# Dilated dynamic filters of layer 1 as matrix products within classes of pixels of equal row and column modulo 6

## The chip, the cores and the metric

The kernel runs on one core of a Trainium2 chip. The metric is device microseconds of one execution. Engines are named as in the profile: PE (TensorE matmul), PEld (its weight loads), DVE (VectorE), ACT (ScalarE), POOL (GpSimd), SP (SyncE, which here only issues DMAs).

## The reference

Four images of 256 channels and 48x48 pixels, all in float32, go through two residual layers. Layer 0 normalizes in groups, convolves 3x3, and applies attention with 8 heads of 32 channels over all 2304 pixels. Layer 1 is what the change concerns. Cut to its core (`gn` is the group-normalized input):

```
guidance = conv3x3(gn, W_cat)                    # 45 planes
outs = [gn]
for i, d in enumerate((1, 6, 12, 24, 36)):
    w = softmax(guidance[:, 9*i : 9*i+9], axis=1)     # 9 weights a pixel
    outs.append(sum over k of shift(gn, dy*d, dx*d) * w[:, k])   # k = (dy, dx), zero outside
y = conv1x1(concat(outs), W_scale)               # 6*256 -> 256 channels
x = x + batchnorm(y)          # statistics over all images
```

The nine weights of a dilation depend on the pixel and are the same for all channels.

## The kernel before, in words

A channel lies on a partition: 256 channels are two halves (`NH`) of 128. An image is cut into six chunks (`NCK`) of eight rows, 384 pixels (`CH`). An outer loop over `b` from 0 to 4 (L1624 onward) alternates two kinds of work. `dynamic_filters(b - 1, ...)` does layer 1 of one image; beside it, as a generator named `other`, runs `conv_qkv(b, ...)`, the convolution and q, k, v of the next image. Then `attention(b, ...)` follows alone. For the last image (`alone`) there is no `other`. I call the three stages with an `other` shared and the last one lone.

The schedule is written out by hand: each engine runs its instructions in program order. The order is chosen by a planner, `Clock` (L645), which holds a time for each engine and is told a cost for each step; `slot` (L663) gives the time at which a buffer is free, and `fill` (L1266) lets PE take filter steps, mixing matmuls from `queue`, or pieces of `other` until a given time. `conv` gives its input transforms (`inputs`, L731) to POOL for all images but the first.

Within `dynamic_filters`:

- `weights` (L1135) makes a chunk's 45 weight planes: a 3x3 convolution on PE (`pg`, L1148, 45 columns, two at a time in two column groups), copies to `lg`, transposes (`pt`), softmax on DVE and ACT (L1188 to L1205), transposes back (`pw`, L1210), a copy to `w` (one in the F32R type and a remainder added in its upper rows), and a store to the DRAM tensor `w_d` on ACT's DMA queue (L1221).
- For each tap (a dilation, a shift) the weight plane must stand on all 128 partitions. Either PE makes it, with a selector column as stationary operand, into a PSUM bank (`wb`, L1432), or the plane is loaded from `w_d` with a broadcasting DMA (`ws`, L1377, ACT's queue) and ACT copies it to PSUM (L1429). `share` and the planner decide; about three fifths go to PE.
- DVE multiplies the bank with the shifted image (`cat` at L1463 for the centre tap, `prod` at L1489 for the others) and POOL adds the product to `cat` (L1506, L1478). Some taps are split between DVE and POOL (L1471 to L1478). In the lone stage some products are mixed without being summed (`single`).
- `mix` (L1294) applies the 1x1 convolution: per dilation and chunk two output halves by two input halves on PE (`py`, L1303). `done` (L1316) copies a finished chunk to SBUF, takes its statistics and stores it to `y_d`.

Taps outside the image are cut away (`taps_of`, L1096). The pixels of a chunk are eight consecutive rows.

At the lone stage's second chunk `back` (L1740) loads the stored `y` and `x1` of earlier images, on SP's queue. `finish` (L1590) scales each image on ACT, adds `x1` on DVE and stores the result on SP's queue, chunk by chunk.

Of the kernel before, what the change touches and what calls it, by code (L numbers as in the profile page):

```python
# [8 lines left out]
F32 = mybir.dt.float32  # L9
# [27 lines left out]
CATS = 4  # L37
PRODS = 6
SLACK = 3000.0
SPLIT = 4500.0  # L40
BEHIND = 0.0
# [7 lines left out]
def conv_preact_kernel(  # L49
# [480 lines left out]
    w_d = tc.dram_tile([B, NCK, NG, CH], F32, name="w_d")  # L530
# [3 lines left out]
    with tc.tile_pool(name="w", bufs=1) as wpool, tc.tile_pool(  # L534
# [22 lines left out]
        pick = wpool.tile([P, NG], F32R, tag="pick", name="pick")  # L557


        e1 = wpool.tile([P, 2 * TPC, 2, 64], F32, tag="e1", name="e1")  # L560
        nc.gpsimd.memset(e1, 0.0)

# [8 lines left out]
        lg = wpool.tile([P, CH], F32, tag="lg", name="lg")  # L571
        nc.gpsimd.memset(lg, 0.0)
# [523 lines left out]
        def taps_of(c, n):  # L1096

            d = DILATIONS[n]
            moves = [(0, 0)] + [
                (sy, sx) for sy in (-1, 0, 1) for sx in (-1, 0, 1) if sy or sx  # L1100
            ]
            for sy, sx in moves:
                oy, ox = sy * d, sx * d
                y0, y1 = max(c * R, -oy), min(c * R + R, HH - oy)
                x0, x1 = max(0, -ox), min(WW, WW - ox)
                if y0 < y1 and x0 < x1:
                    yield 9 * n + 3 * (sy + 1) + sx + 1, oy, ox, y0, y1, x0, x1

        TAP_ELEMENTS = sum(
            NH * (y1 - y0) * (x1 - x0)  # L1110
            for c in range(NCK)
            for n in range(len(DILATIONS))
            for _, _, _, y0, y1, x0, x1 in taps_of(c, n)
        )

        def dynamic_filters(b, ao, chunk, norm, other, pools):


            ps_w, ps_y, ps_m, work1 = pools
            gn = pads[b % 2]  # L1120
            spent = [0.0]
# [12 lines left out]

            def weights(cs):  # L1135


# [4 lines left out]
                for at in range(0, 9 * NH, 3 if pair else 6):  # L1142
                    for i, k in ((at // 9, at % 9 + d) for d in range(3)) if pair else (
                        (0, at // 2 + d) for d in range(3)
                    ):
                        for s in range(2):
# [4 lines left out]
                                window(gn, ii, cc * R, k // 3 - 1, k % 3 - 1),  # L1151
# [12 lines left out]
                for t in range(TPC):  # L1164
                    if pair:
                        nc.tensor.transpose(
                            pt[:, t * P : (t + 1) * P], lg[:, t * P : (t + 1) * P], ident
                        )
                    else:

                        nc.tensor.matmul(
                            pt[:, t * P : t * P + NG], lg[:, t * P : (t + 1) * P],
                            pick.bitcast(F32), start=True, stop=True,
                        )
                lt = pt[:, : TPC * P].rearrange("p (t j) -> p t j", j=64)[:, :, :NG]
                step = 1 if pair else 2
                lt = lt.rearrange("p t (n k) -> p t n k", k=9)[:, ::step]
                ek, ek2 = (
                    e1[:, ::step, j, :NG].rearrange("p t (n k) -> p t n k", k=9) for j in range(2)
                )  # L1180
# [9 lines left out]
                yield 0.0  # L1190
# [7 lines left out]
                yield 0.0  # L1198
                nc.vector.reciprocal(sm, sm)
                clock("DVE", 330)  # L1200
                yield 0.0
                nc.vector.tensor_tensor(ek2, ek, each(sm), ALU.mult)
                clock("DVE", 700)
                yield 0.0
                nc.vector.tensor_tensor(ek, ek, each(sm), ALU.mult)  # L1205
                yield clock("DVE", 1100) + 150
                for s in range(len(cs)):
                    pw = misc(f"pw_{b}_{c + s}")
                    for t in range(TPC):
                        nc.tensor.transpose(  # L1210
                            pw[:, t * P : (t + 1) * P],
                            e1[:, 2 * t + s].rearrange("p a j -> p (a j)"),
                            ident,
                        )

                    w = work1.tile([P, CH], F32R, tag="w", name=f"w_{b}_{c + s}", bufs=3)
                    nc.scalar.copy(w, pw[:, :CH])

                    wf = work1.tile([NG, CH], F32, tag="wf", name=f"wf_{b}_{c + s}", bufs=1)
                    nc.scalar.copy(wf, pw[:NG, :CH])  # L1220
                    nc.scalar.dma_start(out=w_d[b, c + s], in_=wf)  # L1221
                    clock("ACT", 500)
                    yield clock("ACT", 480, clock("PE", 550))
                    nc.vector.tensor_tensor(
                        w[64:], pw[64:, :CH], w[64:].bitcast(F32), ALU.subtract
                    )
                    ready[c + s] = w
                    yield clock("DVE", 560, clock.t["ACT"]) + 150


            alone = b == B - 1
            prods = PRODS - alone
            ready = {}

            def warm(n):
                if alone:
                    busy(misc(f"warm_{b}_{n}"), n)


            while chunk < NCK:  # L1240
                project(b, chunk, ao, ps_y.tile([P, 2, 512], F32, tag="y", name=f"pp_{b}_{chunk}"), norm)
                chunk += 1
            table(AF.Sqrt)
            warm(4)
            run(2400)
            for at, _ in enumerate(norm.finish(misc)):
                run((600, 700)[at])
            table(AF.Exp)
            warm(3)

            for r0, r1 in ((0, 2 * R + 1), (2 * R + 1, HH)):
# [614 lines left out]
```

## Time and profile before

Three runs: 2863.04, 2856.90 and 2862.41 us; the median is 2862.41. The profiled execution is one execution; its span is given here, its own time outside the span is not recorded apart.

| | us |
|---|---|
| median of 3 runs (lowest, highest) | 2862.41 (2856.9, 2863.04) |
| span of the profiled execution | 2861.5 |
| opening: first convolution and q, k, v, to 149.4 | 149.4 |
| four attentions | 378.1, 383.9, 381.5, 377.0 |
| three shared stages | 300.3, 301.3, 300.5 |
| lone stage | 256.0 |
| finish | 33.5 |
| `wb` matmuls in the whole run | 553 records, busy 269.3 |
| `ws` loads | 355, 192 KB each, 3.2 to landing |

How to read it: a group's row gives the instruction's line, engine, tiles, shape and count, then busy time and mean, then idle time before it and what ended that. Busy time of a group is the union of its records, and records of matmuls overlap: an f32 matmul leaves two records, an F32R matmul one.

### The profile page before, as it was taken

Reading aid. Unit: us, or ns where it says so; the run is one execution under the profiler, and the core shown is the slowest. Engines: PE = TensorE matmul, PEld = TensorE weight load, DVE = VectorE, ACT = ScalarE, POOL = GpSimd, SP = SyncE. Lnnn points to the kernel's source line nnn. Section 1 sums busy time; section 2 is a strip of 40 time slices with the busy share of each in tenths; the row PEclk is TensorE's granted clock in tenths of the full one; section 3 lists DMA queues with packets and bytes.
Section 4 is the critical chain, followed back from the end, with each engine's and each line's share of the span. In section 5 each row is a group of like instructions: output and inputs, shape, how many; then the busy total and the mean of one; then the engine's idle time right before and its main releaser. Section 6 shows DMA issues by size and latency. Waiting matters only on the chain. (4 is left out here: it accounts for less than half of the span.)

```text
span 2861.5 us, 43939 instructions
## 1 busy us (share of the span) xinstructions
PE 2703.3 (94%) x16899; PEld 1188.5 (42%) x16899; DVE 2384.4 (83%) x2598; ACT 1707.9 (60%) x2186; POOL 1200.6 (42%) x1036
## 2 busy tenths in 40 slices
PE   7999999999999999999999999999999999998994
PEld 5622223556542222455662222355555222244562
DVE  6588989789878888878987888878986988887886
ACT  3488988422458888722337888852244988871224
POOL 2100010799840010299890010069985001006894
PEclk9999999999999999999999999999999999999997
DMA  5514454233353454333235454424323255435125
GB/s 205 146 34 101 105 106 103 63 115 88 86 120 84 100 106 100 80 90 109 84 86 107 99 105 106 100 68 112 95 77 90 67 106 112 100 81 220 57 74 209
DMA packets 161017, 292.87 MB, mean 102 GB/s; under 512 B 68888, under 2 KB 127072, under 8 KB 159392
## 3 DMA queue, kind: packets, MB, share of 16 engines
q0 software_dynamic: 25568, 135.18, 20.8%
q1 hardware_dynamic: 77776, 80.23, 9.9%
q10 hardware_dynamic: 57456, 74.58, 9.6%
q8 instruction: 135, 2.21, 0.3%
q14 instruction: 82, 0.67, 0.1%
HBM read 134.92 MB, written 32.33 MB: 58 GB/s over the span
## 5 line engine op out<-in xcount | busy, mean ns | idle before, releaser
L1008 DVE TENSOR_TENSOR acc<-acc,p 128x2048 f32<-128x2048 f32 (+1 forms) x572 | 1061.3, 1855 | 116.2 <-ACT p L972 64.8
L972 ACT ACTIVATE p<-se 128x1536 f32<-128x1536 f32 x648 | 938.6, 1448 | 0.0
L1506 POOL TENSOR_TENSOR cat<-cat,prod 128x752 f32<-128x752 f32 (+9 forms) x649 | 868.0, 1346 | 127.4 <-DVE prod L1489 81.3
L963 PE MATMUL so<-q,k 32*128 32x512 f32 (+1 forms) x1440 | 731.0, 595 | 20.1 <-ACT p L971 13.2
L963 PE MATMUL se<-q,k 32*128 32x512 f32 (+1 forms) x4320 | 739.8, 595 | 0.0
L992 PE MATMUL num<-p,vT 128*32 128x512 f32 (+1 forms) x5760 | 705.7, 562 | 4.4 <-ACT p L972 2.4
L1489 DVE TENSOR_TENSOR prod<-wb,pad 128x752 f32<-128x752 f32 (+9 forms) x675 | 474.8, 739 | 79.1 <-PE wb L1432 36.5
L971 ACT ACTIVATE p<-so 128x512 f32<-128x512 f32 x648 | 388.4, 599 | 195.0 <-PE se L963 83.1
L963 PEld LDWEIGHTS so<-q,k 32*128 32x128 f32 x1440 | 217.0, 184 | 539.4 <-ACT p L971 490.0
L1012 POOL DMA_DIRECT2D scratch<-p x124 | 105.6, 852 | 770.1 <-ACT p L972 536.4
L1429 ACT COPY wb<-ws 128x384 f32<-128x384 f32 (+3 forms) x335 | 156.7, 468 | 405.8 <-DVE prod L1489 200.3
L1303 PE MATMUL py<-cat,wsc 128*128 128x384 f32 x960 | 344.6, 490 | 17.5 <-POOL cat L1506 15.0
L992 PEld LDWEIGHTS num<-p,vT 128*32 128x32 f32 x5760 | 133.3, 108 | 479.6 <-issue 446.6
L1432 PE MATMUL wb<-w,pick 128*128 128x384 f32 (+3 forms) x553 | 269.3, 515 | 21.8 <-DVE prod L1489 14.5
L1010 POOL DMA_DIRECT2D scratch<-p x32 | 17.9, 559 | 571.3 <-ACT p L972 387.2
L963 PEld LDWEIGHTS se<-q,k 32*128 32x128 f32 x4320 | 227.6, 184 | 4.4 <-ACT p L972 4.1
L1303 PEld LDWEIGHTS py<-cat,wsc 128*128 128x128 f32 x960 | 174.9, 189 | 124.3 <-POOL cat L1506 30.7
L855 PE MATMUL pc<-cv_q,u 128*128 128x288 f32 x576 | 160.6, 412 | 8.9 <-DVE cv_q L746 6.3
L855 PE MATMUL pc<-cv_k,u 128*128 128x288 f32 x576 | 157.9, 410 | 2.9 <-ACT m L801 2.5
L1148 PE MATMUL pg<-pad,wcat 128*45 128x384 f32 x864 | 157.6, 497 | 3.1 <-DVE pad L595 2.9
L1432 PEld LDWEIGHTS wb<-w,pick 128*128 128x128 f32 x553 | 103.1, 190 | 120.6 <-DVE prod L1489 38.4
L888 PE MATMUL pq<-hid,wqkv 128*128 128x384 f32 x384 | 133.4, 488 | 5.9 <-DVE yt L790 4.8
(229 smaller groups left out, 2360.0 us busy)
## 6 DMA issues: line engine op xcount, KB each, us to landing
scratch<-p POOLq DMA_DIRECT2D x156, 768.0 KB, 5.7
ws<-w_d ACTq DMA_DIRECT2D x355, 192.0 KB, 3.2
pad<-in_x SPq DMA_DIRECT2D x14, 1152.0 KB, 15.5
u<-u_d SPq DMA_DIRECT2D x18, 768.0 KB, 5.3
x_d<-pad SPq DMA_DIRECT2D x48, 192.0 KB, 2.7
xst<-in_x POOLq DMA_DIRECT2D x36, 192.0 KB, 7.9
y_d<-y SPq DMA_DIRECT2D x15, 384.0 KB, 3.6
u_d<-u SPq DMA_DIRECT2D x6, 768.0 KB, 3.8
```

What stands on the lines that cost most here:

```text
L855: nc.tensor.matmul(m, u[:, h, kx, o * P : (o + 1) * P], halves[g][:, h, i, :, kx : kx + WW], start=(h == 0 and kx == 0), stop=(h == NH - 1 ...
L963: nc.tensor.matmul(dst[:, at : at + n], k_[r, g, m * P : (m + 1) * P], q[r, g, q0 : q0 + n], start=True, stop=True,)
L971: nc.scalar.activation(p[:, 0, :], s1, AF.Exp, scale=QS)
L972: nc.scalar.activation(p[:, 1:, :], s3, AF.Exp, scale=QS)
L992: nc.tensor.matmul(st["num"][r, at : at + n], vT[:, m, g * P + j * D : g * P + (j + 1) * D], p[:, j, at : at + n], start=(m == 0 and not s ...
L1008: nc.vector.tensor_tensor(st["acc"][:, js], other[:, js], p[:, js], ALU.add)
L1148: nc.tensor.matmul(pg[64 * s : 64 * s + NG, :CH], wcat[:, ii, k, :], window(gn, ii, cc * R, k // 3 - 1, k % 3 - 1), start=(i == 0 and k == 0),
L1303: nc.tensor.matmul(to, wsc[:, n * NH + i, o * P : (o + 1) * P], rhs(i), start=(n == 0 and i == 0), stop=(last and i == NH - 1),)
L1429: nc.scalar.copy(pw[:, : nr * WW], of[:, : nr * WW])
L1432: nc.tensor.matmul(pw[:, : nr * WW], pick[:, k : k + 1].to_broadcast([P, P]), w[:, l0 * WW : l1 * WW], start=True, stop=True,)
L1489: nc.vector.tensor_tensor(pv, wb, src, ALU.mult)
L1506: nc.gpsimd.tensor_tensor(dst, dst, pv, ALU.add)
```

## The change

**Which pixels belong together.** All far dilations (6, 12, 24, 36) are multiples of 6. A pixel's taps at those dilations all lie in the pixel's own class: rows equal modulo 6, columns equal modulo 6. A class is 8x8 = 64 pixels (`CLS`). A chunk is now every sixth row, so chunk `c` holds six whole classes; two classes make 128 rows, three such pairs (`PAIRS`) a chunk.

**Far dilations** (`far`). For a chunk the image is copied into class order (`own`), turned on PE (`xa`, `xb`: six transposes) and kept as `xT`, pixels on partitions. The weights go through DRAM: the store leaves zero margins in `w_d`, and four small loads per chunk (`loads`) fetch each plane displaced by its tap, so that a row of `wq` holds, for each source pixel, the weight with which it enters its target. Six small matmuls turn them (`wT`). Three predicated copies under masks (`along_x`) spread them over the eight columns of a class (`bmat`), three more (`along_y`) over its eight rows (`amat`): `amat` is then, for each class and dilation, a 64x64 matrix from source to target pixels. Per pair, four matmuls of 64 rows and 256 columns (4 dilations x 64 pixels) give the four dilations' sums, for two channel halves and two classes; the copies that bring them to SBUF (`moved`) go to ACT or DVE, whichever the planner's clock has earlier.

**The near dilation** (`near`) keeps taps: nine per chunk, all on whole rows, as the padded image is read past its edge. Their weights all come by broadcasting DMA and an ACT copy; there is no `wb` matmul. DVE multiplies, POOL adds.

**Order.** Generators `loads`, `far`, `near`, `filters` and `mixes` say when they are due; `drive` takes the first that is due at the clock of PE, and otherwise a piece of `other`. The mixing order in a chunk is the image itself, the four far dilations, the near one.

**Moved.** Weight stores, broadcasts and small loads are issued on SP's queue instead of ACT's. `lg`, `bmat` and `amat` are set to zero by POOL at the start of each image's stage. One half of the normalization goes to ACT. `own` shares its buffer with the chunk's output `y` in the shared stages. Masks are made once, at the start, by POOL. `finish` works on rows that are six apart, and stores images 2 and 3 after their sixth chunk. PSUM: 1 bank for broadcasts and 2 for `far` (lone stage: 2 and 3).

The diff, cut to its core:

```diff
-            ps_w, ps_y, ps_m, work1 = pools
+            ps_w, ps_k, ps_y, ps_m, work1, banks_w, banks_k = pools
...
+            def moved(dst, src, size, *after):
+                if clock.t["ACT"] <= clock.t["DVE"]:
+                    nc.scalar.copy(dst, src)
+                    return clock("ACT", 190 + 0.84 * size, *after)
+                nc.vector.tensor_copy(dst, src)
+                return clock("DVE", 160 + 1.05 * size, *after)
...
+            for t in (lg, bmat, amat):
+                nc.gpsimd.memset(t, 0.0)
...
-                                window(gn, ii, cc * R, k // 3 - 1, k % 3 - 1),
+                                shifted(ii, cc, k // 3 - 1, k % 3 - 1),
...
+                nc.scalar.copy(lg, pw[:, :CH])
...
+                    nc.sync.dma_start(
+                        out=w_d[c + s, :, MARGIN : MARGIN + CH], in_=lg[64 * s : 64 * s + NG]
+                    )
...
+            def loads():
...
+                    for n, d in enumerate(FAR):
...
+                        nc.sync.dma_start(out=t[9 * n : 9 * n + 9, :], in_=a)
...
+            def far():
+                for c in range(NCK):
...
+                    for k in range(STEP):
+                        rows = slice(CLS * (k % 2), CLS * (k % 2 + 1))
+                        at = 9 * NF * (k // 2)
+                        nc.tensor.matmul(
+                            bank[rows, at : at + 9 * NF], wq[:, k], ident[: 9 * NF, : 9 * NF],
+                            start=True, stop=True,
+                        )
...
+                    for t in range(3):
+                        nc.vector.copy_predicated(
+                            bmat,
+                            along_x[:, :, t, :].bitcast(mybir.dt.uint32).unsqueeze(1).to_broadcast(
+                                [P, PAIRS, 3 * NF, SIDE]
+                            ),
+                            wT[:, :, :, t].unsqueeze(3).to_broadcast([P, PAIRS, 3 * NF, SIDE]),
+                        )
+                        end = clock("DVE", 460, end)
...
+                        nc.vector.copy_predicated(
+                            amat,
...
+                        end = clock("DVE", 960)
...
+                    for p in range(PAIRS):
...
+                        for h in range(NH):
+                            for s in range(2):
+                                rows = slice(CLS * s, CLS * (s + 1))
+                                nc.tensor.matmul(
+                                    two[s][:, h * C : (h + 1) * C],
+                                    xT[rows, p, h * P : (h + 1) * P],
+                                    amat[rows, NF * p : NF * (p + 1)].rearrange(
+                                        "p n j i -> p (n j i)"
+                                    ),
+                                    start=True,
+                                    stop=True,
+                                )
+                        clock("PE", 950)
+                        for s in range(2):
...
+                            done_at = moved(
+                                dst, two[s].rearrange("p (k m) -> p k m", m=CLS), 512,
+                                clock.t["PE"],
+                            )
...
+            def near():
...
+                    fetch(number + WBS)
...
+                    nc.scalar.copy(pw[:, :CH], fetched[c, k][0])
...
+                    nc.gpsimd.tensor_tensor(cat, cat, prod, ALU.add)
...
-                        nc.tensor.matmul(
-                            pw[:, : nr * WW],
-                            pick[:, k : k + 1].to_broadcast([P, P]),
-                            w[:, l0 * WW : l1 * WW],
-                            start=True,
-                            stop=True,
-                        )
...
+            def mixes():
+                order = (0, *range(2, 2 + NF), 1)
+                for c in range(NCK):
+                    now[0] = c
+                    if alone and c == 1:
+                        back()
...
+            def drive(streams):
...
+                        if d <= clock.t["PE"]:
+                            due[j] = next(streams[j], None)
+                            break
+                        soonest = min(soonest, d)
+                    else:
+                        got = next(other, None)
...
+            streams = [
+                loads(), far(), near(), filters([(0,), (1,), (2, 3), (4, 5)]), mixes(),
+            ]
...
             for b, ty, tx in ((2, y_2, x1_2), (3, homes, x1_3)):
                 for c in range(NCK):
...
-                    nc.sync.dma_start(out=image_of(out, b)[:, :, cols], in_=ty[c])
...
+                for o in range(NH):
+                    for cols in (slice(0, N // 2), slice(N // 2, N)):
+                        nc.sync.dma_start(out=image(b, o)[:, cols], in_=tx[:, o, cols])
```

## The prediction

> **What bounds the kernel now.** I read the page's totals first, then busy time by stage, then the waits of a stage, then single stretches of the timeline.
>
> ```profile
> PE 2703.3 (94%) x16899; PEld 1188.5 (42%) x16899; DVE 2384.4 (83%) x2598; ACT 1707.9 (60%) x2186; POOL 1200.6 (42%) x1036
> ```
>
> PE carries the run. A limit is read by stage, though. The table cuts the span at the first score matmul of each attention and at its last projection; columns are PE, PEld, DVE, ACT, POOL busy, then PE clock, DMA share, GB/s.
>
> ```profile
> core 0: us, PE busy (x) PEld busy (x) DVE busy (x) ACT busy (x) POOL busy (x), PEclk, DMA share, GB/s
> 149.40:527.50 378.10, 370.98 (x3017) 105.71 (x3017) 331.04 (x218) 330.06 (x354) 40.75 (x46) 0.99 0.40 87
> 1211.70:1513.00 301.30, 286.20 (x1147) 178.02 (x1145) 248.57 (x396) 88.72 (x182) 272.12 (x211) 1.00 0.34 90
> 2572.00:2828.00 256.00, 232.85 (x922) 138.59 (x920) 201.87 (x327) 49.65 (x106) 206.37 (x166) 0.97 0.35 117
> 2828.00:2861.50 33.50, 0.00 (x0) 0.00 (x0) 23.70 (x31) 25.98 (x38) 0.00 (x0) 0.52 0.83 309
> ```
>
> The first row is an attention, which the change leaves alone (four of them, with the opening 149.4 us). The second is one of three *shared* stages: layer 1 of an image with layer 0 of the next on PE, PE 95% busy. The third is the *lone* stage, layer 1 of the last image with nothing beside it. The fourth is the finish. Only the last three kinds can change. Next, what PE waits for in a shared stage:
>
> ```profile
> PE py L1303 <- POOL cat L1506: 5.2, 8, 1.1
> PE wb L1432 <- DVE prod L1489: 3.2, 5, 1.1
> PE so L963 <- DVE bound L926: 2.0, 1, 2.0
> ```
>
> Idle is 15.1 us, 8.4 of it on tap sums and products: PE's own work sets the stage's length. Last, what one broadcast costs PE (start, length):
>
> ```profile
> 656.74 1.46 PE L1303 MATMUL py<-pad,wsc 128*128 128x384 f32 x4
> 658.03 2.74 PE L1303 MATMUL py<-cat,wsc 128*128 128x384 f32 x8
> 660.32 0.63 PE L1432 MATMUL wb<-w,pick 128*128 128x384 f32 x1
> 660.79 1.13 PE L855 MATMUL pc<-cv_q,u 128*128 128x288 f32 x4
> ```
>
> Start to start, 4 mixing records take 1.29 us, so 8 take 2.58; eight and one broadcast take 2.76. A broadcast adds 0.18 us, though its record says 0.63. Records overlap; starts are the measure. An f32 matmul leaves two records.
>
> [...] in attention 16 records of 32 rows and 256 columns, four heads side by side, take 1.07 us from 499.57 to 500.64 in slots of 0.21 to 0.32. [...] a POOL add of 128x600 goes from 1.46 to 2.14 us while DVE normalizes (1217 to 1226). [...]
>
> ```profile
> L1506 POOL TENSOR_TENSOR cat<-cat,prod 128x768 f32<-128x768 f32 x114 | 208.0, 1825 | 10.2 <-DVE prod L1489 1.5
> L1489 DVE TENSOR_TENSOR prod<-wb,pad 128x768 f32<-128x768 f32 x120 | 113.9, 949 | 12.5 <-ACT wb L1429 4.9 <-POOL cat L1506 3.9 <-PE wb L1432 3.0
> L1429 ACT COPY wb<-ws 128x384 f32<-128x384 f32 x304 | 146.8, 483 | 357.7 <-DVE prod L1489 181.5 <-DMA ws<-w_d 83.3 <-DVE cat L1463 47.0
> ```
>
> **PE in a shared stage.** What stays, by starts in gap-free stretches: 288 conv records at 0.2425 us (24 in 5.82) are 69.8; 96 qk at 0.3225 are 31.0; 72 v at 0.2175 are 15.7; 288 mixing at 0.3225 are 92.9; 216 filter records at 0.169 (36 in 6.08) are 36.5; transposes of logits and weights 5.6. Sum 251.5. Busy is 286.2, so 134 broadcasts with the switches around them hold **34.7 us**, all removed (134 x 0.18 = 24 is the floor).
>
> Added, per image: 18 groups of four K=64 matmuls, two row halves side by side. Each is four slots of 0.215 [...], like the attention stretch: 1.07, sum 19.3. Were the halves not parallel, it would be 8 slots, 1.9 each, 34.8. 36 transposes at 0.167 (18 `pw` records are 3.00 busy) are 6.0. 36 matmuls of 36 columns, 72 records at 0.1 (6 `pt` records start to start about 0.6), are 7.2. Sum **32.5**, between 27 and 51. Mixing is the same 144 matmuls. So -2 net.
>
> Waits: the 8.4 us on tap sums go; new ones stand on copies of the far results (three PSUM groups of a chunk pass through two banks). DVE falls to about 150 us of 300 and POOL from 272 to about 140 (48 adds of 1.83 and some 50 of conv inputs), so I take -2, between -8 and +15. POOL's queue: three memsets per image now stand ahead of the conv inputs, and wait for attention's buffers. Inputs begin at 1203 now; attention's last DVE step ends at 1207.1. With 1.3 us of memset (448 ns for 128x384) they begin at 1208.4 and the first conv matmul moves from 1211.6 to about 1214: +2 (0 to 3). ACT broadcasts fall from 88 to 54 and are hidden. A shared stage: -2; **three: -6** (-36 to +36).
>
> **The lone stage.** Here the chain counts. From 2572: PE's filter convolution ends near 15 us, `pw` at 20 as now; copy 0.5, store 1.8, four small loads' issues and landing about 5: the first `wT` at 28. Three predicated copies of 288 and three of 768 follow, priced as tensor_tensor of the size (0.45 and 0.95): 4.2; doubled they are 8.4; below that I see no reason for. With chunk 1's softmax between, far group 0 runs at 35. PE is full meanwhile: far groups with filters of chunks 2 and 3 to 50, mixing of far 0 (16 matmuls, 10.3, and transposes) to 62, filters of 4 and 5 (12.2) to 74, then far 1, near 0, own 1 and turning chunk 2 to 85.5.
>
> From then a chunk's period is the longer of two. PE: 10.3 + 2.6 + 2.6 of mixing, 3.2 far groups, 2 turning: 20.7. Chain: copies and statistics 5.3, then in DVE's order the next near products, whose 8 POOL adds take 14.6 behind a first product of 0.95, then half a mix 1.3, turning 2: **24.2**. Three periods reach 158; near, own and far mixing 14.2, the last far group 10, far mixing 10.3, near and statistics 4.6: end near **198 instead of 256: -58**. Bounds: PE alone -75; copies doubled on the chain in six chunks, -33.
>
> On SP's queue the weight broadcasts now stand behind 11.8 MB of loads that `back` issues at about 52 us (at the 420 GB/s that such loads reach at 2580 to 2610: 28 us). Chunk 2's are wanted at about 115: hidden; uncovered 28.
>
> **Finish and start.** ACT does about 27 us of scaling (25.98 now), but the last image's 2.36 MB go out after its sixth chunk instead of chunk by chunk: at 390 GB/s 6 us and a landing of 2 to 3, against 6.4 now from ACT's last end. Row: **+5** (2 to 8). At the start, 72 tiny POOL copies and 12 small stores lie in a POOL that is 27 us busy in 149: 0; uncovered they delay statistics by about 9 us that PE wants only at 123.
>
> **Sum.** 2861.5 - 6 - 58 + 5 = 2802.5 in the profiled execution; the median of the runs is 0.9 above its span: **2803 us**.
>
> **Rivals.**
> 1. The lone stage shrinks half as much: predicated copies at half speed, or `back`'s loads in the way. For: no row shows that copy; the queue is shared. Against: the cover of 60 us above. 256 to 228, total 2833.
> 2. The shared stages gain too: -34.7 in full against 27, and the 8.4 us of waits go. For: DVE and POOL have half their time free. -12 each: 2862.4 - 36 - 58 + 5 = 2773.
> 3. Slower: PE waits at every far group, because DVE's half of the copies stands in its queue behind up to two products (2 x 0.95 = 1.9). For: two banks, in-order queue. Against: ACT takes the other half, and conv matmuls stand between groups. 18 x 3 x 1.9 = 103, so 2906. It decides from 59/54 = 1.1 us a group.
>
> That the broadcasts stay is excluded: the new instruction order has no `wb` matmul.
>
> **Chances.** Forecast 0.50, rival 1 0.18, rival 2 0.18, rival 3 0.14. The range 2765 to 2850 takes in the first three and leaves out most of rival 3 and a tail. Within 0.2% (6 us, about what can be told from no change) 0.03, slower 0.13, faster 0.84, since rival 3 passes through no change when its wait is near 1.1 us.
>
> **What would show it.** Stages of 298 and 198 us and a finish of 38; PE busy in a shared stage near 284; far groups about 1.07 us; predicated copies of 0.45 and 0.95. Wrong if a far group takes 1.9, if the copies take double, if PE's waits in a shared stage exceed 25 us, or if the lone stage stands on `ws` landings.

## The result, and the profile after

The changed kernel takes 2794.07 us (median of 4 runs, 2793.82 to 2797.24). Beside it the kernel before took 2861.09 (4 runs, 2856.9 to 2863.04). The ratio is 0.9772, with a 95% interval of 0.9758 to 0.9786. The forecast was 2803, in a range of 2765 to 2850. The profiled execution has a span of 2791.9 us. First the page's totals.

```profile
PE 2647.6 (95%) x17122; PEld 1140.7 (41%) x17122; DVE 2024.1 (72%) x1948; ACT 1771.8 (63%) x2175; POOL 632.1 (23%) x583
```

PE still carries the run. Over the whole run it is 56 us less busy, DVE 360 and POOL 568. Now the stages. To compare them I cut both spans by one rule: a shared stage runs from the start of an attention's last projection to the next attention's first score matmul, and the lone stage ends where the scale of the final normalization starts (`ysc_f`). Rows of before cut in this way come first: the second shared stage, lone stage, finish. (The prediction's shared row was cut 1.5 us later.)

```profile
core 0: us, PE busy (x) PEld busy (x) DVE busy (x) ACT busy (x) POOL busy (x), PEclk, DMA share, GB/s
1211.20:1511.40 300.20, 285.10 (x1140) 177.97 (x1139) 248.57 (x396) 88.72 (x182) 272.55 (x212) 1.00 0.33 90
2571.60:2828.20 256.60, 233.25 (x923) 138.81 (x921) 202.03 (x328) 49.65 (x106) 206.37 (x166) 0.97 0.35 117
2828.20:2861.50 33.30, 0.00 (x0) 0.00 (x0) 23.53 (x30) 25.98 (x38) 0.00 (x0) 0.51 0.83 309
```

The same stages of the changed kernel:

```profile
1198.30:1490.40 292.10, 285.65 (x1253) 176.06 (x1251) 154.87 (x229) 102.74 (x175) 119.54 (x72) 1.00 0.33 81
2539.10:2752.30 213.20, 182.23 (x810) 98.00 (x808) 122.17 (x171) 68.62 (x113) 87.04 (x48) 0.95 0.41 128
2752.30:2791.90 39.60, 0.00 (x0) 0.00 (x0) 24.39 (x33) 26.81 (x41) 0.00 (x0) 0.53 0.70 271
```

In the shared stage PE is as busy as before (285.1, then 285.7), but its idle time went from 15.1 to 6.5 us. In the lone stage PE's work fell by 51 us and the stage by 43. The account of the span:

| | before, us | after, us | difference | forecast |
|---|---|---|---|---|
| opening | 149.4 | 149.8 | +0.4 | 0 |
| four attentions | 377.6, 384.3, 382.6, 377.3 | 376.5, 379.9, 380.1, 377.2 | -8.1 | 0 |
| three shared stages | 299.9, 300.2, 300.3 | 292.1, 292.1, 291.4 | -24.8 | -6 |
| lone stage | 256.6 | 213.2 | -43.4 | -58 |
| finish | 33.3 | 39.6 | +6.3 | +5 |
| span | 2861.5 | 2791.9 | -69.6 | -59 |

What PE waits for in the second shared stage after the change (total us, times, longest us):

```profile
PE pw L1244 <- DVE e L1240: 2.2, 2, 1.8
PE pg L1190 <- DVE pad L631: 1.4, 1, 1.4
PE pc L891 <- POOL cv_q L782: 1.2, 1, 1.2
PE xa L1307 <- ACT own L1163: 1.1, 1, 1.1
```

The rows on tap sums (5.2 us) and products (3.2) are gone, and so is the one on `bound` (2.0). No row on far results has come in their place. The end of the same stage tells more. Before the change PE ends it with the last tap sums of layer 1 and then has nothing to do until the bound is there:

```profile
1504.83 0.49 PE L1303 MATMUL py<-cat,wsc 128*128 128x384 f32 x1
1506.45 2.85 PE L1303 MATMUL py<-cat,wsc 128*128 128x384 f32 x8 [1.13 <-POOL cat L1506]
1509.13 0.28 PE L925 MATMUL pb<-qktop,hmat 128*128 128x2 f32 x2
1511.40 0.99 PE L963 MATMUL so<-q,k 32*128 32x512 f32 x1 [1.99 <-DVE bound L926]
```

After the change it ends with the next image's v matmuls, and the first scores follow at once:

```profile
1484.79 5.56 PE L945 MATMUL pv<-wqkv,hid 128*128 128x256 f32 x25
1490.19 0.28 PE L961 MATMUL pb<-qktop,hmat 128*128 128x2 f32 x2
1490.40 1.12 PE L999 MATMUL so<-q,k 32*128 32x512 f32 x2
```

Layer 1, with POOL busy for 272 of 300 us, used to end last; now layer 0 does, which is PE's own work.

In the lone stage most of the 51 us are mixing. Three rows give the instructions of one tile alone: the mixing (`py`) before, the broadcasts (`wb`) before, and the mixing after (length of the stage, then busy time and count of PE, PEld, DVE and ACT):

```profile
2571.60:2828.20 256.60, 163.73 (x496) 89.85 (x496) 1.13 (x2) 4.94 (x7) 0.97 0.35 117
2571.60:2828.20 256.60, 70.17 (x151) 27.97 (x151) 171.25 (x264) 33.16 (x71) 0.97 0.35 117
2539.10:2752.30 213.20, 102.87 (x288) 54.31 (x288) 1.13 (x2) 4.95 (x7) 0.95 0.41 128
```

Before, products of this stage were mixed without being summed first, so the mixing took 496 records; now it takes 288, as in a shared stage, which is 61 us less. The 151 broadcasts are gone too. Their records overlap those of their neighbours; what the other groups leave of PE's busy time is an estimate of 16 us for them. The same subtraction gives 29 us for the new steps after the change. With 3 us less in small groups that is -61 -16 +29 -3, the 51 us.

PE waits in this stage for:

```profile
PE pw L1244 <- DVE e L1240: 5.0, 3, 3.2
PE wT L1337 <- DMA wq<-w_d: 4.5, 2, 2.4
PE far L1387 <- ACT far L1163: 4.5, 6, 0.8
PE py L1536 <- ACT yu L1493: 2.7, 3, 0.9
PE py L1536 <- POOLq L1899: 2.0, 1, 2.0
```

No single wait is large: the 31 us of PE's idle time in this stage are spread over some 28 short ones. Finally the groups that the prediction had to price without a row:

```profile
L1163 ACT COPY far<-far 128x512 f32<-128x512 f32 x82 | 87.9, 1099 | 125.1 <-PE far L1387 125.1
L1359 DVE COPY_PREDICATED amat<-along_y,bmat 128x768 f32<-128x768 uint32 x72 | 75.2, 1044 | 1.9
L1165 DVE COPY far<-far 128x512 f32<-128x512 f32 x62 | 67.8, 1093 | 69.1 <-PE far L1387 69.1
L1347 DVE COPY_PREDICATED bmat<-along_x,wT 128x288 f32<-128x288 uint32 x72 | 34.5, 480 | 18.4 <-PE wT L1337 16.7
```

The predicated copies cost 0.48 and 1.04 us (forecast 0.45 and 0.95, the prices of products of 288 and 768 values: 449 and 949 ns in the kernel before, L1489). A copy of 512 far values costs 1.1 us on either engine; the prediction did not price it, and the planner is told 0.62 on ACT and 0.70 on DVE.

### The profile page after: what moved, and what is told of

Read it like the earlier page. It is cut to its first block, busy times and chain, and to the rows that moved or that the text cites. A ratio compares the mean times of both kernels' runs of the same rounds, so it can differ in the third digit from the quotient of the medians.

```text
span 2791.9 us, 42246 instructions
## 1 busy us (share of the span) xinstructions
PE 2647.6 (95%) x17122; PEld 1140.7 (41%) x17122; DVE 2024.1 (72%) x1948; ACT 1771.8 (63%) x2175; POOL 632.1 (23%) x583
## 5 line engine op out<-in xcount | busy, mean ns | idle before, releaser
L1007 ACT ACTIVATE p<-so 128x512 f32<-128x512 f32 x648 | 388.8, 600 | 182.2 <-PE se L999 72.8
L1458 POOL TENSOR_TENSOR near<-near,prod 128x768 f32<-128x768 f32 x192 | 348.4, 1815 | 402.5 <-DVE prod L1453 390.8
L1536 PE MATMUL py<-far,wsc 128*128 128x384 f32 x768 | 255.2, 487 | 0.0
L1453 DVE TENSOR_TENSOR prod<-wb,pad 128x768 f32<-128x768 f32 x192 | 182.3, 955 | 99.2 <-ACT wb L1440 59.1
L1440 ACT COPY wb<-ws 128x384 f32<-128x384 f32 x216 | 107.8, 501 | 210.7 <-DVE prod L1453 192.0
L1536 PEld LDWEIGHTS py<-far,wsc 128*128 128x128 f32 x768 | 144.0, 190 | 99.2 <-issue 3.7
L1163 ACT COPY far<-far 128x512 f32<-128x512 f32 x82 | 87.9, 1099 | 125.1 <-PE far L1387 125.1
L891 PE MATMUL pc<-cv_q,u 128*128 128x288 f32 x576 | 153.9, 414 | 9.0 <-DVE cv_q L782 6.2
L1190 PE MATMUL pg<-pad,wcat 128*45 128x384 f32 x864 | 151.7, 496 | 8.2 <-DVE pad L631 4.8
L891 PEld LDWEIGHTS pc<-cv_q,u 128*128 128x128 f32 x576 | 107.5, 191 | 46.6 <-DVE cv_q L782 6.3
L924 PE MATMUL pq<-hid,wqkv 128*128 128x384 f32 x384 | 125.3, 487 | 1.1 <-ACT q L931 0.6
```

The source lines that it names most:

```text
L891: nc.tensor.matmul(m, u[:, h, kx, o * P : (o + 1) * P], halves[g][:, h, i, :, kx : kx + WW], start=(h == 0 and kx == 0), stop=(h == NH - 1 ...
L924: nc.tensor.matmul(pq[:, :CH], wqkv[:, i, s, g * P : (g + 1) * P], hid[:, i, cols], start=(i == 0), stop=(i == NH - 1),)
L1007: nc.scalar.activation(p[:, 0, :], s1, AF.Exp, scale=QS)
L1190: nc.tensor.matmul(pg[64 * s : 64 * s + NG, :CH], wcat[:, ii, k, :], shifted(ii, cc, k // 3 - 1, k % 3 - 1), start=(i == 0 and k == 0), st ...
L1440: nc.scalar.copy(pw[:, :CH], fetched[c, k][0])
L1453: nc.vector.tensor_tensor(prod.rearrange("p h (r w) -> p h r w", w=WW), wb, src, ALU.mult)
```

## Experiments

Each run is the changed kernel with one edit, unless more are named. Times are medians of 4 runs (5 for the last), stage lengths come from the profiled execution by the rule above. Between kernels with the same code in a stage, shared stages differ by 1 us at most, the lone stage by about 1.5 (4 in one run, `pool`), an attention by up to 5.

### What took the waits out of the shared stages

Run `pool` loads POOL as before the change:

```
-                    nc.gpsimd.tensor_tensor(cat, cat, prod, ALU.add)
+                    again = not alone and k != 0
+                    for op in (ALU.add, ALU.subtract, ALU.add)[: 3 if again else 1]:
+                        nc.gpsimd.tensor_tensor(cat, cat, prod, op)
```

> The changed kernel with POOL loaded in the shared stages about as it was before the change: seven of eight near taps are added, subtracted and added again (84 more adds of 1.8 us per image, POOL from 119 to some 272 us busy per shared stage, as before); the lone stage is untouched. If the 9 us that each shared stage gained came from POOL's shorter queue (before, PE waited 5.3 us per stage for tap sums), each shared stage goes back by 5 us or more: 297 instead of 291.6, and 2809 in total. If it came from DVE's shorter queue, or from PE having no broadcasts in its own queue any more, the stages stay within 1.5 us of 291.6 and the total is 2794 to 2798.

Measured: 3236.08 us (ratio to before 1.1319, 1.13 to 1.1338); shared stages of 437.6, 438.5 and 436.8.

Run `dve` makes each near product of the shared stages three times (`for _ in range(1 if alone else 3)` around the product).

> The changed kernel with DVE loaded in the shared stages as before the change: each near product is made three times over (96 more products of 0.95 us per image, DVE from 155 to about 246 us per shared stage; before it was 248.6); the lone stage is untouched. If DVE's shorter queue brought the gain (before, PE waited about 8 us per stage for DVE results: products, bound, yt), each shared stage goes back by 4 us or more: 296 and 2806 in total. If POOL's queue did, or the absence of broadcasts in PE's own queue, the stages stay within 1.5 us of 291.6: 2794 to 2798.

Measured: 3042.79 us (1.0642, 1.0624 to 1.0659); shared stages of 372.0, 374.1 and 372.0.

Both are far outside every expectation. The planner did not know of the added work, and so placed mixing where its sums were not ready: of these two runs nothing can be read on a gain of 8 us. The next two add to these edits the cost that the planner is told, `clock("POOL", 5400 if again else 1800, end)` and `clock("DVE", 960 if alone else 2800, ...)`.

> The run with POOL loaded by 84 more adds per image again, but now the planner that orders PE's work is told their cost (5400 in place of 1800 ns). Before, untold, it placed the near mixing too early and PE stood 205 us for near sums, which says nothing on the gain. If POOL's shorter queue brought the 8 us of a shared stage, the stages go back by 5 us or more, to 297 to 300, total 2810 to 2818. If not, they stay within 2 us of 292.5, total 2794 to 2800.

Measured: 3104.41 us (1.0858, 1.0842 to 1.0875); shared stages of 392.8, 393.0 and 393.2.

> The run with DVE loaded by 96 more products per image again, but now the planner is told their cost (2800 in place of 960 ns). Untold, PE stood 80 us for far copies and 48 for near sums. If DVE's shorter queue brought the 8 us of a shared stage, the stages go back by 4 us or more, to 296 to 300, total 2806 to 2818. If not, they stay within 2 us of 292.5, total 2794 to 2800. If both this run and the one with POOL stay, the gain comes from PE's own queue, which has no broadcast any more that waits for a product.

Measured: 3029.88 us (1.0591, 1.0575 to 1.0608); shared stages of 369.0, 368.6 and 369.8.

Here POOL's timeline in the first shared stage of `pool2`:

```profile
639.08 20.89 POOL L1460 TENSOR_TENSOR near<-near,prod 128x768 f32<-128x768 f32 x11
720.07 60.36 POOL L1460 TENSOR_TENSOR near<-near,prod 128x768 f32<-128x768 f32 x32 [60.10 <-DVE prod L1453]
```

For 60 us POOL has no product to add while PE runs through the rest of the next image's layer 0 (its q, k and v matmuls end at 728). After that no piece of `other` is left to fill in, and PE waits for near sums, 70 us in the stage (42 in `dve2`): layer 1 ends last again, as before the change, but with its work bunched at the end. So under this planner a load on POOL or on DVE alone is enough to make layer 1 end last. More can't be read from the four runs: the stages grew by 77 to 101 us, ten times the gain, and POOL, loaded as before the change, stood idle for 60 us because of the order of the work. What took out the 8 us is read from the waits alone. Of the waits that are gone, 3.7 us were those of broadcasts, which stood in PE's queue for a product or a sum on DVE (3.2 and 0.5); such a wait can't occur where PE makes no broadcast. The others were waits of other matmuls for POOL's sums (5.2) and for DVE (4.4). That lighter queues on these two engines are what removed them is likely, but not shown, and how they divide stays open.

### The lone stage: predicated copies and the loads beside them

Run `pred` makes each predicated copy of the lone stage twice (same values):

```
-                    for t in range(3):
+                    for t in (0, 1, 2) * (1 + alone):
...
-                    for t in range(3):
+                    for t in (0, 0, 1, 1, 2, 2) if alone else range(3):
```

> The changed kernel with every predicated copy of the lone stage made twice (18 x 0.48 and 18 x 1.02 us more on DVE: 4.5 us per chunk, 27 in all). The prediction put these copies on the chain of each chunk: lone stage 213 + 27 = 240, total 2821, up to 2827. The rival, read off the trace afterwards, is that from chunk 2 on PE's own order sets the period and the copies lie beside it: only the first chunk's copies are waited for, lone stage 213 + 4 to 8, total 2798 to 2802.

Measured: 2841.63 us (0.9935, 0.9919 to 0.9952); lone stage 262.4, 49 more than the changed kernel's 213.2, above both theories. The copies are not the only thing in it; a wait on DMA is too. That wait shows most plainly in the run `near`, which moves two of eight adds of a chunk from POOL to DVE:

```
+                    if alone and k in (0, 3):
+                        held_prod = prod
+                        continue
+                    if alone and k in (1, 5):
+                        nc.vector.tensor_tensor(prod, prod, held_prod, ALU.add)
```

> The changed kernel with two of eight POOL adds per chunk of the lone stage taken over by DVE (products of taps 0 and 1, and of 3 and 5, are added on DVE first): POOL 14.5 to 10.9 us per chunk, DVE 1.9 us more. The prediction said that the chain through these adds sets the period of a chunk (24.2 us against 20.7 of PE): then each of four chunks is 1.7 to 3.6 us shorter, lone stage 199 to 206, total 2780 to 2787. Rival: PE's own order with its small waits sets it (PE does not wait for near sums before the last chunk): 0 to -2, total 2792 to 2794.

Measured: 2808.84 us (0.9816, 0.98 to 0.9833); lone stage 231.4, slower by 18 where both theories had it faster or equal. ACT's timeline in that stage (start, length):

```profile
2646.08 0.48 ACT L1440 COPY wb<-ws 128x384 f32<-128x384 f32 x1 [1.43 <-DVE prod L1453]
2669.60 0.94 ACT L1440 COPY wb<-ws 128x384 f32<-128x384 f32 x2 [23.04 <-DMA ws<-w_d]
2672.39 1.07 ACT L1163 COPY far<-far 128x512 f32<-128x512 f32 x1
```

and PE's:

```profile
2656.24 0.70 PE L1387 MATMUL far<-amat,xT 64*128 64x256 f32 x2
2673.51 2.07 PE L1387 MATMUL far<-amat,xT 64*128 64x256 f32 x6 [16.58 <-ACT far L1163]
```

ACT stands 23 us for one weight broadcast, because `back` had issued its 11.8 MB some 3 us before it; the far copies are queued behind it on ACT, and PE stands 16.6 us for them. In `pred` it is the same, 22.9 us on ACT and 15.0 on PE. In the changed kernel itself the largest such wait is 4.7 us. That is the prediction's "uncovered 28": the cover was there, but in the order that the planner makes of 2 us more DVE work per chunk it is gone. How many microseconds it is thick was not measured. On the near adds, `near` shows no gain outside the stall: 231.4 less 16.6 is 214.8.

Run `spread` takes the loads apart:

```
-                    if alone and c == 1:
-                        back()
+                    if alone and c >= 1:
+                        back(c)                # one load of 2.36 MB for each of chunks 1 to 5
```

> The changed kernel with the 11.8 MB that the lone stage loads for the finish issued one load (2.36 MB) at the start of each of chunks 1 to 5, not all at chunk 1. The prediction called them hidden. Theory: they are not quite; weight rows and broadcasts land late behind them (PE waits 2.4 us for the weight rows of chunk 3, ACT 9.4 us for broadcasts), and the clock falls to 0.79 after it: lone stage 3 us shorter, total 2791. Rival: hidden; the total stays at 2794 within 1.5, or the late loads delay the finish by 1 to 3 us.

Measured: 2789.66 us (0.9759, 0.9743 to 0.9775); lone stage 210.4, finish 39.6 as it was. The 2.8 us are what was expected, though only just beyond the spread of that stage, and ACT has no wait on a broadcast left among its seven largest. Now the copies can be priced without the loads, with both edits in `predspread`:

> Every predicated copy of the lone stage made twice, with the 11.8 MB of loads spread over chunks 1 to 5. In the run with the loads in one piece the lone stage took 262 us, 49 more, but 31 of them were two stalls in which ACT and POOL waited for broadcasts that landed behind these loads. Against 210.4 us with spread loads and single copies: theory of the prediction, copies on the chain of all six chunks: +27 to +33, lone stage 237 to 243, total 2814 to 2820. Rival, on the path in the first chunks only while PE's own order covers the rest: +5 to +18, lone stage 215 to 228, total 2792 to 2806.

Measured: 2827.05 us (0.9884, 0.9869 to 0.9899); lone stage 243.8, which is 33.4 more than `spread`. This is the prediction's size, but not its picture. Counted from the stage's start, the class transposes (`wT`) of chunks 3 and 5 begin at 114.6 and 164.6 in `spread`, at 138.8 and 185.5 in `predspread`: 24.2 us are lost before chunk 3, 3.3 won up to chunk 5, 12.5 lost after it. PE's waits in the stage:

```profile
PE py L1536 <- POOL near L1458: 23.9, 3, 16.2
PE pw L1244 <- DVE e L1240: 10.1, 3, 4.7
PE far L1387 <- ACT far L1163: 4.5, 6, 0.8
```

Waits on far copies stay at 4.5 us, those on near sums go from 2.0 to 23.9, those on softmax from 5.0 to 10.1. The copies delay the near products, and with them eight adds of 1.8 us a chunk, more than the far results. But DVE was not full. The same stretch of `predspread` and of `spread`, and POOL's adds in `predspread`:

```profile
2598.00:2636.00 38.00, 29.04 (x164) 14.75 (x163) 27.68 (x44) 8.32 (x14) 1.92 (x2) 0.92 0.07 18
2598.00:2636.00 38.00, 36.19 (x179) 18.75 (x178) 26.64 (x39) 13.76 (x25) 21.89 (x13) 1.00 0.49 140
2635.89 20.55 POOL L1458 TENSOR_TENSOR near<-near,prod 128x768 f32<-128x768 f32 x11 [35.76 <-DVE prod L1453]
```

DVE is busy for 27.7 of these 38 us, and for 26.6 in `spread`. Yet POOL stands idle for 35.8 us, because the planner, which is told the cost of the copies, has put chunk 0's near products behind the copies of two more chunks. The longest wait on near sums, 16.2 us, follows from that. So the 33.4 us are the price of the copies together with a new order; that they meet the forecast's size is luck, and the price of the copies in an unchanged order was not measured.

### The start of the lone stage

Run `soft` holds the large predicated copies of chunk 0 back until chunk 1's weights are on their way:

```
+                    if alone and c == 0:
+                        yield lambda: 0.0 if 1 in stored else NEVER
                     for t in range(3):
                         yield lambda: clock.t["DVE"] - 600
```

> The changed kernel with one step moved in the lone stage: the three large predicated copies of chunk 0 come after chunk 1's softmax on DVE, not before and within it. Theory: the forecast's lone stage was 6 us short at its start because PE stands for 5 us at this softmax (3.2 us on the weights of chunk 1, 1.2 us on the flag) and then runs its next 12 records at half clock (4.08 instead of 2.16 us); with the softmax first, PE starts its filters 3 us earlier: lone stage 208 to 210, total 2789 to 2791. Rival: the far results of chunk 0 are what the start waits for; they come 2 us later, and the lone stage ends 0 to 2 us later: 2794 to 2796.

Measured: 2789.67 us (0.975, 0.9734 to 0.9767); lone stage 208.7, so 4.5 shorter, as the theory had it. Its reason is not confirmed: PE still waits 3.2 us for this softmax and 1.9 for the flag, and the filters start 8.1 us after the first `wT`, not 7.3 as in the changed kernel. What the edit did was to let near products of chunk 0 pass the copies: POOL's first add comes 35.8 us after the stage's start, in place of 61.8. Nor does the gain arise at the start: only 1.1 of the 4.5 us is there at the class transposes of chunk 4 (137.8 us after the start, in place of 138.8), 2.6 at those of chunk 5, and the rest comes in the tail. The near mixing at 2679 that runs at half clock in the changed kernel (8 records in 5.02 us, see below) runs at full speed here, while here the far mixing at 2657 is slow in its place (32 records in 12.80 us, not 10.48). That the earlier near sums are worth 4.5 us is an inference, not shown.

### The far copies

Run `read` writes far results in the order in which they come, and lets PE read them in pixel order:

```
-                            dst = cat.rearrange("p h n (m b) -> p (h n) m b", b=STEP)[
-                                :, :, :, 2 * p + s
+                            dst = cat.rearrange("p h n (b m) -> p (h n) b m", b=STEP)[
+                                :, :, 2 * p + s, :
...
-                                    rhs = far_done[c][0][:, i, n - 2, :]
+                                    rhs = far_done[c][0][:, i, n - 2, :].rearrange(
+                                        "p (b m) -> p m b", b=STEP
+                                    )
```

> The changed kernel with the far results written to SBUF in the order in which they come (runs of 64 values) and read in pixel order by the mixing matmuls (a stride of 64 values); the same values are computed. Theory: the copies of 128x512 take 1.10 us because they write with a stride of six values; then they fall to about 0.6 us, the 4.5 us that PE waits for them in the lone stage go, and with them some of the waits behind: lone stage 207 to 209, shared stages unchanged, total 2789. Rival a: the copies keep 1.10 us, since it is their PSUM side or their shape that costs: 2794. Rival b: strided reading slows the mixing; at one tenth more for the 768 far records this is 25 us: 2815.

Measured: 3025.39 us (1.0574, 1.0557 to 1.0592). Three groups of its page:

```profile
L1538 PE MATMUL py<-far,wsc 128*128 128x384 f32 x768 | 506.5, 827 | 0.0
L1163 ACT COPY far<-far 128x512 f32<-128x512 f32 x82 | 47.0, 586 | 326.7 <-PE far L1387 326.7
L1165 DVE COPY far<-far 128x512 f32<-128x512 f32 x62 | 42.8, 690 | 267.4 <-PE far L1387 267.4
```

The stride is the whole surcharge: the copies fall from 1.10 to 0.59 and 0.69 us. But the far mixing matmuls double: 32 records take 20.96 us in place of 10.48. Per shared stage that is 60 us, and it swamps the gain. Paying on ACT and DVE, where there is room, is the better of the two.

### The finish, and the edits together

Run `fin` does images 2 and 3 by halves of the channels:

```
-                for c in range(NCK):
-                    for o in range(NH):
-                        scaled(ty[c][:, o], o)
+                for o in range(NH):
+                    for c in range(NCK):
+                        scaled(ty[c][:, o], o)
```

with the add of `x1` cut to one half and the stores of a half moved into the outer loop.

> The changed kernel with images 2 and 3 of the finish done one half of the channels after the other (scaling, adding and storing 1.18 MB before the second half), instead of chunk by chunk with all 2.36 MB stored after the sixth chunk. The prediction's finish grew by 5 us because the last image leaves in one piece: then the finish falls from 39.6 to 36 or 37 us, total 2791. Rival: the scaling on ACT and 24 adds in place of 12 on DVE fill the finish, and nothing is gained: 2793 to 2796.

Measured: 2789.24 us (0.9757, 0.9741 to 0.9773); finish 36.0 instead of 39.6, so 3.6 of the 6.3 us are those of the last piece.

> The changed kernel with three of the edits together, but not the strided reading: chunk 1's softmax ahead of the large predicated copies of chunk 0, the loads of the lone stage spread over its chunks, and images 2 and 3 of the finish done one half of the channels after the other. Alone they took 4.5 us, 2.8 us off the lone stage and 3.6 us off the finish. If they are independent: lone stage 206, finish 36, total 2782 to 2784. Rival: the softmax edit and the spread loads remove the same waits (both shift the first two chunks against the landing of weight rows), so only the larger of them counts: 2785 to 2787.

This kernel holds the strided reading of `read` as well as the three edits, so its expectation does not apply. Measured: 3018.79 us (1.0555, 1.054 to 1.0569). It can only be read against `read`: lone stage 259.6 instead of 267.4, finish 36.8 instead of 39.4, together 10.4 us, where the three edits alone had 4.5, 2.8 and 3.6 (10.9). That speaks for independent gains. Their sum on the changed kernel, some 2783 us, was not measured. Each of the three edits alone had a median 4.4 to 4.8 us below the changed kernel's; the intervals of the ratios overlap, so it is the stage lengths that carry these gains.

## Why the prediction was right

Most of the gain comes from the stages that were named. That the total came within 9 us is luck, since errors of both signs cancel: the shared stages and the attentions gave 27 us more than forecast, the lone stage 15 less. By its steps:

**PE in a shared stage: right.** Forecast -2 net; by the common cut PE's busy time went up by 0.6 us, to 285.7 (forecast near 284). A far group takes 1.07 us (one starts at 672.81, the next instruction at 673.88), as forecast: the two row halves do run side by side (four slots of 0.215 are 0.86, eight one after the other would be 1.72; what the other 0.21 us are is not shown). 12 records of `wT` take 0.80 us, 6 transposes 0.80; with 19.3 for far groups the additions come to 28.9 us by starts. By the forecast's own subtraction (285.7 less 251.5 for what stays) they are 34.2, which includes whatever else lies around them. Both lie inside the forecast's 27 to 51.

**The waits of a shared stage: the direction right, the term mis-sized.** The forecast let 8.4 us go and new ones come, -2 net, with +2 for the memsets ahead of the convolution's inputs: 0 in all. Measured: -8.7. What goes is more, 13.3 us: tap sums and products 8.9, `yt` 2.4 and `bound` 2.0, which also stood on DVE. What comes is 5.0: softmax 1.8 more, `pad` 0.5, the convolution's first input 1.2, `own` 1.1, `wT` 0.4. The far copies, for which the forecast had booked most of the new waits, cost nothing here, since other matmuls stand between far groups. The memsets were about right: they take 1.3 us, POOL starts its first input behind them at 1195.8, and PE's first convolution matmul waits 1.2 us for it (forecast 2). Rival 2 (-12 each) erred on the other side: it is -8.3 each, in the mean.

**The lone stage: the mechanism right in part, 15 us short.** PE's own work was right: the bound "PE alone -75" leaves 181 us, and PE is busy for 182.2 (the prediction does not say that most of what falls away is mixing). The chain beside it was not. The marks from the stage's start:

| | forecast, us | measured, us | new delay |
|---|---|---|---|
| first `wT` | 28 | 29.8 | 1.8 |
| first far group | 35 | 41.2 | 4.4 |
| `wT` of chunk 2 | 85.5 | 91.8 | 0.1 |
| `wT` of chunk 5 | 158 | 167.4 | 3.1 |
| end | 198 | 213.2 | 5.8 |

The stretch before the first far group, on PE:

```profile
2568.92 0.88 PE L1337 MATMUL wT<-ident,wq 36*64 36x36 f32 x12 [2.14 <-DMA wq<-w_d]
2569.73 0.87 PE L1213 MATMUL pt<-pick,lg 128*128 128x45 f32 x6
2573.78 0.87 PE L1244 MATMUL pw<-ident,e 128*128 128x128 f32 x3 [3.18 <-DVE e L1240]
2575.81 0.20 PE L1678 MATMUL pf<-okay,one 128*1 128x8 f32 x2 [1.16 <-DVE okay L1675]
2576.25 4.08 PE L1190 MATMUL pg<-pad,wcat 128*45 128x384 f32 x12 [0.24 <-DVE count L1680]
2580.26 1.37 PE L1387 MATMUL far<-amat,xT 64*128 64x256 f32 x8
```

Two things were missing in the forecast. The flag by which the kernel checks its attention bounds (`okay`, `count`) is computed just here, and PE waits for it (1.2 and 0.2 us). And the granted clock is down: it was 0.50 in 2571.6 to 2579.6, and the next 12 filter records take 4.08 us, where 12 take 2.16 a few microseconds on. It fell at 2570.5, and the longest gap of PE in the 5 us before was 2.1 us; it is full again at 2580.8, after 4.5 us of steady work. It is down once more from 2676.4 to 2683.2 (0.57 in the 8 us from 2675.6): it fell in the last of three gaps of 0.75, 0.75 and 1.43 us, and came back after 6.7 us of steady work. What lowers the clock in these two places is left open. The stage's mean clock is 0.95 against 0.97 before.

In the middle, the three periods took 24.9, 22.2 and 28.5 us, mean 25.2 against the forecast's 24.2. The size was right; the reason given, that POOL's eight adds set the period, is not seen: before the last chunk PE waits for no near sum, and two adds fewer brought no gain that shows. In its place stand PE's own 20.7 us, a handful of waits below 1.5 us, on far copies (0.75 each when groups follow each other), on `own` and on the PSUM pair of the mixing, one wait of 2.4 us for the weight rows of chunk 3, and the half clock near 2680. The tail is longer because near sums and their copy are waited for (2.0 and 1.2 us) and its parts come out 1 to 3 us above their prices.

The cover of `back`'s loads was right for this kernel (2.8 us, by `spread`), but the prediction's "60 us above" was too comfortable: it put the loads at 52 us into the stage and the use of chunk 2's broadcasts at 115. The loads are issued at 85 us in the changed kernel and at 97 in `near`, where ACT wants chunk 2's first broadcast at 108. (The 420 GB/s of its estimate hold for 2582 to 2605; the whole stretch from 2580 to 2610 that it names has 377.)

**Rival 1** named doubled copies at -33 us of gain: `predspread` gives 33.4, by another path and with another order of the work. It did not come true because the copies run at about the speed of ordinary operations (0.48 and 1.04 us against 0.45 and 0.95 for products of these sizes). **Rival 3** needed 1.1 us a far group: it is 0 in shared stages and 0.25 in the lone stage (4.5 over 18).

**The finish: right**, +6.3 for +5, and `fin` takes back 3.6 by the cause named.

**The attentions** were forecast at 0 and gave 8 us, most of it in the second and third. In the second, PE's waits on the exponentials fall from 6.9 to 3.6 us; why is left open. In `pool2` and `dve2` the second and third take 381 to 382 us again, in the other runs 378 to 380.5; that fits a load from the stage before, but the spread of an attention is of the same size.

## What to carry to other kernels

When work is taken off the engines beside the bound one, read the gain from that engine's list of waits, row by row, and don't book new waits where other work stands between the new steps. For a load called hidden, ask how much shift its cover bears, and split a long one: in `near` one broadcast behind 11.8 MB held ACT's queue for 23 us. Where a planner orders the work, an experiment that adds work measures the new plan as much as the work, whether the planner is told (`predspread`) or not (`pool`): look at what the engines do in the stretch before you read the number as a price.

## What was not expected of the hardware

- Copies of 128x512 from PSUM to SBUF with a stride of six float32 values take 1.10 us on ACT and 1.09 on DVE, contiguous 0.59 and 0.69. A float32 matmul whose moving operand is read from SBUF with a stride of 64 values takes twice as long (32 records 20.96 us against 10.48). Other strides were not measured, and why these cost what they do is left open.
- A predicated copy with broadcast operands costs about as much as an ordinary operation of its size on DVE: 0.48 us for 288 values, 1.04 for 768 (a product of 288 took 0.449 in the kernel before, one of 768 takes 0.955).
- In the lone stage of the changed kernel the granted clock fell to 0.50 after gaps of PE of at most 2.1 us in one place and 1.43 us in another, and came back after 4.5 and 6.7 us of steady work.
